# Two graph-attention and expert layers on one core: the first layer's row terms sent through DRAM, and two of four norms taken from accumulator sums and squares on ScalarE

## The chip, the cores and the metric

The kernel runs on one core of one Trainium2 chip, as one launch. The metric is the device time of that launch in microseconds (us). The kernel before took 1596.94 us (the median of three runs, 1593.39 to 1600.9). One further execution was taken with the hardware profiler; every line number, duration and wait below comes from it.

Five engines are named as in the profile: PE (TensorE, with its weight load PEld), DVE (VectorE), ACT (ScalarE), POOL (GpSimd) and SP (SyncE, which here only issues transfers). Each executes its own instructions in the order in which they were recorded.

## What is computed

x holds 64 batches of 256 rows with 256 features, float32. The adjacency (256 x 256) is the same for all batches. Two layers follow each other; cut to what matters:

```python
# layer 0: attention of 4 heads (64 wide), then a linear map
h = layernorm(x);  q = (h @ W).reshape(B, N, 4, 64)
e = leaky(e_src[:, :, None, :] + e_dst[:, None, :, :], 0.2)   # e_src, e_dst = q @ a
attn = softmax(where(adj > 0, e, -9e15), axis=2)
x = x + elu(einsum('bijh,bjhd->bihd', attn, q))
x = x + layernorm(x) @ weight.T + bias
# layer 1: attention of 1 head, then a mixture of 8 experts, 2 per row
x = x + relu(softmax(mask(leaky(...))) @ (layernorm(x) @ W))
t = layernorm(x);  top-2 experts of t @ router_w.T
x = t + sum over the two of weight * (gelu(t @ w1 + b1) @ w2 + b2)
```

The softmax weights need no exponential of a 256 x 256 matrix: exp(leaky(s + d)) is a maximum of two products, so each entry of the weights is max(row term, column term) times the mask, and the denominator comes from a column of ones-like terms in the product with q. The row terms of a head are 256 numbers that every partition needs: one number for each row i, the same on all 128 partitions (which carry j). How these numbers get to all partitions is the first thing changed here. The mean and the variance of the four layernorms of a batch are the second.

## The kernel before

**Work of a batch.** `batch_layers` (line 509) is a Python generator: it records the instructions of one batch in some twenty pieces, and between two pieces it yields a rank. A loop at the end of the file (line 1112 on) goes through steps. In every step it takes each active generator once, in the order of the ranks that they yielded, and lets it record its next piece; a negative rank means a further piece in the same step. Three steps (`TICKS = 3`) are one period, and a new batch begins in each period, so in a steady state one period holds one complete batch's work, made up of pieces of some seven batches. The recorded order is the order on every engine; nothing reorders it later. Engines wait for each other only by semaphores.

**Order of a batch's pieces (before):** blocks of x turned on DVE (L116); norm of x (L374, L375, finished on POOL by L382 and L383); projection on PE (L405) and exponentials on ACT (L413); `scaled` on DVE (L421) in the same step; in the next two steps `scores` for heads 0, 1 and heads 2, 3; then `attended` on PE (L496); the head products divided (on ACT, L534, for batches under `EARLY = 16`, else on DVE, L539); the ELU: `e` on ACT (L545), x1 on DVE (L548, L549); x1b (L552: POOL for the early batches, else DVE); norm of x1, transposed on PE (L389) and copied by ACT (L395); the linear map on PE (L560) and x2 on DVE (L566); norm of x2; transposed, copied, projected for layer 1 (L440), ACT exponentials (L447, L448, L453); scores of layer 1 (L459, L464), attention (L496), `rel` on ACT (L582); x2 += rel on DVE (L586); its norm; normalised rows on ACT (L603, L608), stored by SP (L619), transposed, router logits on PE (L633). A batch's routing and its experts follow in other generators: rows are scattered to DRAM by POOL (L933), read back in pairs of 128 rows by SP (L767, L793), turned (L116 sT), multiplied (L825), passed through gelu on ACT (L831), multiplied again (L840), biased on DVE (L850), weighted on ACT (L818) and added to the output by POOL (L861). Three batches at the end take a dense way.

**Row terms before.** `scores` (line 469) lets PE transpose a column of q that is broadcast along the free axis, once for each head and half (L475, eight 128 x 128 transposes for a batch, in two groups of four). The result lies in a PSUM bank `pd` on all partitions. DVE then forms the weights `z` of a head and a half from `pd`, a column of q and the mask (L482, eight instructions of 128 x 256 for a batch).

**Norms before.** `norm_stats` (line 360) issues two BATCH_NORM_STATS2 (L374) and two BATCH_NORM_AGGREGATE (L375) on DVE for each of the four norms of a batch. Two norms that fall into one step share one pair of POOL instructions, which add EPS and raise to the power -1/2 (`finish_norms`, L382 and L383).

**Transfers.** In the steady state all are issued by SP and POOL; ACT issues six at the start and none after. Every transfer takes one of eight completion semaphores in turn, and waits for the transfer that had it before.

Of the kernel before, what the change touches and what calls it, by code (L numbers as in the profile page):

```python
# [9 lines left out]
F32 = mybir.dt.float32  # L10
# [5 lines left out]
P = 128  # L16
# [11 lines left out]
def kernel(  # L28
# [83 lines left out]
    S = 32  # L112

# [270 lines left out]

    def transposed(src, pool=work, tag="xT", bufs=4, blocks=False):
        pt = bank("pt", [KT, N])
        for t in range(NT):
            for k in range(KT):
                nc.tensor.transpose(  # L389
                    pt[:, k, t * P : (t + 1) * P],  # L390
                    by_block(src[:, t, :])[:, k] if blocks else src[:, t, k * P : (k + 1) * P],
                    ident,
                )
        dst = pool.tile([P, KT, N], F32, tag=tag, name="xT", bufs=bufs)
        nc.scalar.copy(dst, pt)  # L395
        return dst
# [59 lines left out]
    def scores1(ex, me):  # L456
        pd = bank("pd", [N])
        for t in range(NT):
            nc.tensor.transpose(  # L459
                pd[:, t * P : (t + 1) * P], ex[:, t, 1:2].to_broadcast([P, P]), ident  # L460
            )
        z = work.tile([P, NT, N], F32, tag="z", name="z", bufs=6)
        for j in range(NT):
            nc.vector.scalar_tensor_tensor(  # L464
                z[:, j, :], pd, ex[:, j, 2:3], me[:, j, :], op0=ALU.max, op1=ALU.mult
            )
        return z

    def scores(q, heads, hs, mask, probs):

        d = D // heads
        pd = bank("pd", [len(hs), N])
        for i, h in enumerate(hs):
            for t in range(NT):
                nc.tensor.transpose(  # L475
                    pd[:, i, t * P : (t + 1) * P],
                    q[:, t, h, d + 1 : d + 2].to_broadcast([P, P]), ident,
                )
        for i, h in enumerate(hs):
            z = work.tile([P, NT, N], F32, tag="z", name="z", bufs=6)  # L480
            for j in range(NT):
                nc.vector.scalar_tensor_tensor(  # L482
                    z[:, j, :], pd[:, i, :], q[:, j, h, d + 2 : d + 3], mask[:, j, :],
                    op0=ALU.max, op1=ALU.mult,
                )
            probs.append(z)

    def attended(q, heads, probs):
# [3 lines left out]
        for t in range(NT):  # L492
            pv = bank("pv", [heads, d + 1])
            for h, z in enumerate(probs):
                for j in range(NT):
                    nc.tensor.matmul(  # L496
                        pv[:, h, :], z[:, j, t * P : (t + 1) * P], q[:, j, h, : d + 1],
                        start=(j == 0), stop=(j == NT - 1),
                    )
# [6 lines left out]
    def batch_layers(b, c0, xng, lg):  # L506
# [13 lines left out]
        scaled(q, pqs, H, rstd)  # L520
        yield 10
        probs = []
        scores(q, H, range(0, 2), masks[0], probs)
        yield 10
        scores(q, H, range(2, 4), masks[0], probs)
        yield 50
        pvs, rinv = attended(q, H, probs)
# [36 lines left out]
        x2 = work.tile([P, NT, D], F32, tag="x2", name="x2", bufs=4)  # L564
        for t in range(NT):
            nc.vector.scalar_tensor_tensor(  # L566
                x2[:, t, :], pf[:, t, :], rstd[:, t : t + 1], x1b[:, t, :],
                op0=ALU.mult, op1=ALU.add,
            )
        _, rstd = norm_stats(x2)  # L570
# [7 lines left out]
        pvs, rinv = attended(q[:, :, None, :], 1, [z])  # L578
        yield 5
        rel = work.tile([P, NT, D], F32, tag="rel", name="rel", bufs=1)  # L580
        for t, pv in enumerate(pvs):
# [4 lines left out]
        nc.vector.tensor_add(x2, x2, rel)  # L586
        mv, rstd = norm_stats(x2)
        yield 15
# [3 lines left out]
            by[:, 0], mv[:, :, 0], -1.0, rstd, op0=ALU.mult, op1=ALU.mult  # L592
# [512 lines left out]
    with tc.manual_schedule():  # L1105
        while more or active or waiting or dense_jobs or scatters:
# [35 lines left out]
            if half_done:  # L1142
                finish_norms(NT)
            active[:] = [a for a in active if a[0] is not None]
# [36 lines left out]
```

## Time and profile before

| | |
|---|---|
| median of three runs | 1596.94 us (1593.39 to 1600.9) |
| the profiled execution: its time, its span | 1597.13 us, 1595.3 us |
| mean granted PE clock | 0.977 |
| transfers | 207.58 MB, 361512 packets |
| L475 transposes of q, PE | 512, busy 77.5 us |
| L482 z, DVE | 512, 473 ns each |
| L374, L375 of all four norms, DVE | 512 each, busy 156.2 + 50.5 and 93.1 us |
| L545 e, ACT | 64, 642 ns each |
| ACT table loads of 1283 ns | 66 + 49 + 6 + 4 + 3 + 3 + 1 |

Busy time counts the time in which an engine executes; register, semaphore and transfer-issuing instructions are not in it. Instructions that overlap on one engine are counted once within a group, and groups of one engine can overlap each other, so the groups' busy times add up to more than the engine's. In the timeline a row gives the start, the length, engine, line, operation, the tile written and read, the count of merged instructions, and in brackets the engine's idle time ahead of it and what ended it. "SPq" and "ACTq" rows are the issuing of transfers on these engines' queues.

### The profile page before, as it was taken

Reading aid. Unit: us, or ns where it says so; the run is one execution under the profiler, and the core shown is the slowest. Engines: PE = TensorE matmul, PEld = TensorE weight load, DVE = VectorE, ACT = ScalarE, POOL = GpSimd, SP = SyncE. Lnnn points to the kernel's source line nnn. Section 1 sums busy time; section 2 is a strip of 40 time slices with the busy share of each in tenths; the row PEclk is TensorE's granted clock in tenths of the full one; section 3 lists DMA queues with packets and bytes.
Section 4 is the critical chain, followed back from the end, with each engine's and each line's share of the span. In section 5 each row is a group of like instructions: output and inputs, shape, how many; then the busy total and the mean of one; then the engine's idle time right before and its main releaser. Section 6 shows DMA issues by size and latency. Waiting matters only on the chain. (4 is left out here: it accounts for less than half of the span.)

```text
span 1595.3 us, 30506 instructions
## 1 busy us (share of the span) xinstructions
PE 1493.9 (94%) x8570; PEld 1317.6 (83%) x8570; DVE 1325.8 (83%) x4473; ACT 902.8 (57%) x2003; POOL 903.3 (57%) x867
## 2 busy tenths in 40 slices
PE   6998888999999999999999999999898997769998
PEld 5887777888888888888888888888787886658886
DVE  6898988989898989898998989899898889655553
ACT  2455455466666656666665666666466776544332
POOL 2332636265757666666757575756755575654443
PEclk9999998999999999999999999999999999889999
DMA  5712223456666667565666666666576665678863
GB/s 160 207 50 55 85 73 90 116 134 140 133 140 144 132 149 147 121 148 131 153 130 154 132 131 138 144 140 139 124 160 128 124 143 105 134 187 164 155 120 47
DMA packets 361512, 207.58 MB, mean 130 GB/s; under 512 B 261497, under 2 KB 331649, under 8 KB 361345
## 3 DMA queue, kind: packets, MB, share of 16 engines
q1 hardware_dynamic: 311488, 138.31, 35.6%
q0 software_dynamic: 48864, 66.33, 22.8%
q8 instruction: 71, 1.16, 0.3%
q10 hardware_dynamic: 992, 0.99, 0.2%
q14 instruction: 97, 0.79, 0.2%
HBM read 117.43 MB, written 88.09 MB: 129 GB/s over the span
## 5 line engine op out<-in xcount | busy, mean ns | idle before, releaser
L861 POOL DMA_INDIRECT out_dram<-y,xt x258 | 411.8, 1596 | 182.1 <-ACT hT L831 50.5
L496 PE MATMUL pv<-q,z 128*128 128x65 f32 (+1 forms) x2560 | 372.8, 301 | 5.7 <-issue 4.4
L496 PEld LDWEIGHTS pv<-q,z 128*128 128x128 f32 x2560 | 333.9, 194 | 19.1 <-issue 4.6
L840 PE MATMUL py<-w2s,hT 128*128 (+1 forms) x1224 | 283.5, 383 | 7.8 <-ACT hT L831 6.5
L382 POOL TENSOR_SCALAR rstd<-mv 128x4 f32<-128x4 f32 (+1 forms) x132 | 57.0, 432 | 411.0 <-DVE mv L375 365.0
L933 POOL DMA_INDIRECT xs<-xng,pos x244 | 247.7, 1015 | 65.4 <-issue 63.1
L840 PEld LDWEIGHTS py<-w2s,hT 128*128 128x128 f32 x1224 | 229.6, 192 | 40.4 <-ACT hT L831 9.3
L395 ACT COPY xT<-pt 128x512 f32<-128x512 f32 x192 | 113.4, 591 | 253.9 <-PE pt L389 189.6
L825 PE MATMUL ph<-sT,we 128*128 128x256 f32 x1032 | 241.1, 384 | 10.9 <-DVE sT L116 10.0
L825 PEld LDWEIGHTS ph<-sT,we 128*128 128x128 f32 x1032 | 193.5, 193 | 36.9 <-DVE sT L116 10.8
L482 DVE SCALAR_TENSOR_TENSOR z<-pd,q,mask 128x256 f32<-128x256 f32 x512 | 210.9, 473 | 0.0
L831 ACT ACTIVATE hT<-ph,we 128x256 f32<-128x256 f32 x306 | 127.7, 470 | 143.0 <-PE ph L825 120.0
L818 ACT ACTIVATE y<-y,w 128x256 f32<-128x256 f32 x258 | 112.5, 500 | 135.8 <-DVE y L850 115.2
L383 POOL TENSOR_TENSOR rstd<-rstd,mhalf 128x4 f32<-128x4 f32 (+1 forms) x132 | 161.2, 1221 | 11.0
L374 DVE BATCH_NORM_STATS2 stats<-x 128x6 f32<-128x256 f32 x384 | 156.2, 407 | 2.2
L440 PE MATMUL pq<-wx,xT 128*128 128x259 f32 x512 | 129.5, 394 | 24.3 <-ACT xT L395 13.0
L405 PE MATMUL pq<-wx,xT 128*128 128x268 f32 x512 | 132.8, 404 | 5.7 <-DVE xT L116 3.8
L850 DVE TENSOR_TENSOR y<-py,b2s 128x512 f32<-128x512 f32 x129 | 85.9, 686 | 60.6 <-PE py L840 44.9
L440 PEld LDWEIGHTS pq<-wx,xT 128*128 128x128 f32 x512 | 91.7, 189 | 51.6 <-ACT xT L395 22.7
L560 PE MATMUL pf<-wfT,xT 128*128 128x256 f32 x512 | 123.3, 384 | 0.1
L405 PEld LDWEIGHTS pq<-wx,xT 128*128 128x128 f32 x512 | 98.3, 196 | 24.8 <-issue 3.2
L375 DVE BATCH_NORM_AGGREGATE mv<-stats 128x2 f32<-128x6 f32 x512 | 93.1, 182 | 17.5
(159 smaller groups left out, 2339.7 us busy)
## 6 DMA issues: line engine op xcount, KB each, us to landing
we<-wpack SPq DMA_DIRECT2D x145, 288.0 KB
xr<-xs SPq DMA_DIRECT2D x516, 64.0 KB
xblk<-in_x_dram SPq DMA_DIRECT2D x256, 64.0 KB
xin<-in_x_dram SPq DMA_DIRECT2D x64, 256.0 KB
out_dram<-base SPq DMA_DIRECT2D x61, 256.0 KB
out_dram<-y,xt POOLq DMA_INDIRECT x258
xs<-xng,pos POOLq DMA_INDIRECT x244
xs<-fill SPq DMA_DIRECT2D x9, 260.0 KB
```

The lines of the kernel that those rows point to most:

```text
L374: nc.vector.bn_stats(stats[:, t, :], src[:, t, :])
L383: nc.gpsimd.tensor_tensor(rstd[:, :n], rstd[:, :n], mhalf[:, :n], ALU.pow)
L405: nc.tensor.matmul(pq.rearrange("p h c -> p (h c)"), xT[:, k, t * P : (t + 1) * P], wx[:, k, :], start=(k == 0), stop=(k == KT - 1),)
L440: nc.tensor.matmul(pq, xT[:, k, t * P : (t + 1) * P], wx1[:, k, :], start=(k == 0), stop=(k == KT - 1),)
L482: nc.vector.scalar_tensor_tensor(z[:, j, :], pd[:, i, :], q[:, j, h, d + 2 : d + 3], mask[:, j, :], op0=ALU.max, op1=ALU.mult,)
L496: nc.tensor.matmul(pv[:, h, :], z[:, j, t * P : (t + 1) * P], q[:, j, h, : d + 1], start=(j == 0), stop=(j == NT - 1),)
L560: nc.tensor.matmul(pf[:, t, :], xT[:, k, t * P : (t + 1) * P], wfT[:, k, :], start=(k == 0), stop=(k == KT - 1),)
L825: nc.tensor.matmul(ph[:, f, :], we[:, k * D + f * P : k * D + (f + 1) * P], xT[:, k, :], start=(k == 0), stop=(k == KT - 1),)
L831: nc.scalar.activation(hT[:, f, :], ph[:, f, :], AF.Gelu, bias=we[:, C_B1 + f : C_B1 + f + 1])
L840: nc.tensor.matmul(py[:, t, :], hT[:, f, t * P : (t + 1) * P], w2s[:, e, f * D : (f + 1) * D].rearrange("p e c -> p (e c)"), start=(f == 0 ...
L861: d = nc.gpsimd.indirect_dma_start(out=out_rows, out_offset=bass.IndirectOffsetOnAxis(ap=xt[:, t, 0:1].bitcast(I32), axis=0), in_=y[:, t, ...
L933: d = nc.gpsimd.indirect_dma_start(out=xs_d[: E * CAP * PAIR, :], out_offset=bass.IndirectOffsetOnAxis(ap=at, axis=0), in_=xe, in_offset=None,
```

## The change

In layer 0 the row terms no longer pass through PE. `send_terms`: DVE transposes the 32 columns that hold them (4 for each of 8 head-halves) in blocks of 32 x 32 into `ut`; ACT issues a transfer of the 32 rows that matter, 128 bytes each, to a small DRAM tile, 4 KB for a batch. Two steps later `spread_terms`: ACT issues one transfer that reads these 4 KB for each of the 128 partitions, 512 KB in SBUF, into the second half of a new tile `z4` (two buffers). Two steps after that `scores` runs, now with both large operands in SBUF: it multiplies in place, the last half over the row terms themselves. Between `scaled` and `scores` there are four steps in place of one, so all later pieces of a batch are recorded one period later relative to its projection; the program has three steps more.

The norm of x2 and that after x2 += rel no longer use BATCH_NORM_STATS2. The DVE instructions that produce x2 now also give the sum of each row (`accum_out`), the addition of `rel` is split into two halves for it, and ACT computes Square(sum - 256 x) with an accumulator for each half: four activations of 128 x 256 for a batch, which write their elements into one scratch tile `off` with one buffer. POOL turns the accumulators into 1/sqrt as before, with its own pairing. `by` is formed from the sums, and is recorded at rank 80 instead of 15. The other two norms (of x and of x1) stay as they were.

On ACT the four squares come, in the recorded order, after the copy of the transposed normalised rows (L395, xT<-pt) and ahead of `e` (L545); the transfer of the terms is issued right behind the squares. The spreading transfer is issued behind the copy of the transposed x1. On PE the two groups L475 vanish and nothing else moves within a period.

```diff
+    G = P // S
+    def norm_squares(src, sums):
+        ...
+        for t in range(NT):
+            off = work.tile([P, D], F32, tag="off", name="off", bufs=1)
+            nc.scalar.activation(
+                off, src[:, t, :], AF.Square, bias=sums[:, t : t + 1], scale=-float(D),
+                accum_out=sq[:, at + t : at + t + 1],
+            )
+        if at:
+            finish_squares(2 * NT)
+        return rstd[:, at : at + NT]
+
+    def finish_squares(n):
+        sq, rstd = half_squared.pop()
+        nc.gpsimd.tensor_scalar(
+            rstd[:, :n], sq[:, :n], 1.0 / D**3, EPS, op0=ALU.mult, op1=ALU.add
+        )
+        nc.gpsimd.tensor_tensor(rstd[:, :n], rstd[:, :n], mhalf[:, :n], ALU.pow)
...
+    def send_terms(q, b):
+        ut = small.tile([P, S], F32, tag="ut", name="ut", bufs=1)
+        nc.vector.transpose(
+            ut.rearrange("p (t h w) -> p t h w", t=NT, h=H), q[:, :, :, HD - 1 : HD + 3]
+        )
+        ud = tc.dram_tile([S, S], F32, name=f"terms_{b}")
+        ud = ud.rearrange("c r -> (c r)").rearrange("(c p) -> c p", p=P)
+        return ut, ud
+
+    def spread_terms(ud):
+        z = work.tile([P, NT, NT, H, P], F32, tag="z4", name="z4", bufs=2)
+        nc.scalar.dma_start(
+            out=z[:, NT - 1].rearrange("p t h i -> p (t h i)"),
+            in_=rows_to_all(ud, S * S),
+        )
         return z
 
-    def scores(q, heads, hs, mask, probs):
-        pd = bank("pd", [len(hs), N])
-        for i, h in enumerate(hs):
-            for t in range(NT):
-                nc.tensor.transpose(
-                    pd[:, i, t * P : (t + 1) * P],
-                    q[:, t, h, d + 1 : d + 2].to_broadcast([P, P]), ident,
-                )
-        for i, h in enumerate(hs):
-            z = work.tile([P, NT, N], F32, tag="z", name="z", bufs=6)
+    def scores(q, z, hs):
+        for h in hs:
             for j in range(NT):
                 nc.vector.scalar_tensor_tensor(
-                    z[:, j, :], pd[:, i, :], q[:, j, h, d + 2 : d + 3], mask[:, j, :],
+                    z[:, j, :, h, :], z[:, NT - 1, :, h, :], q[:, j, h, HD + 2 : HD + 3],
+                    masks[0][:, j, :].rearrange("p (t i) -> p t i", t=NT),
                     op0=ALU.max, op1=ALU.mult,
                 )
...
         scaled(q, pqs, H, rstd)
+        ut, ud = send_terms(q, b)
+        yield -75
+        nc.scalar.dma_start(
+            out=ud.rearrange("c (g r) -> g c r", g=G),
+            in_=ut[2 : P : S // (NT * H), :],
+        )
+        yield 99
+        yield 30
+        z = spread_terms(ud)
+        yield 99
         yield 10
-        probs = []
-        scores(q, H, range(0, 2), masks[0], probs)
+        scores(q, z, range(0, 2))
         yield 10
-        scores(q, H, range(2, 4), masks[0], probs)
+        scores(q, z, range(2, 4))
         yield 50
...
         x2 = work.tile([P, NT, D], F32, tag="x2", name="x2", bufs=4)
+        sums = row_sums()
         for t in range(NT):
             nc.vector.scalar_tensor_tensor(
                 x2[:, t, :], pf[:, t, :], rstd[:, t : t + 1], x1b[:, t, :],
-                op0=ALU.mult, op1=ALU.add,
-            )
-        _, rstd = norm_stats(x2)
+                op0=ALU.mult, op1=ALU.add, accum_out=sums[:, t : t + 1],
+            )
+        rstd = norm_squares(x2, sums)
...
-        nc.vector.tensor_add(x2, x2, rel)
-        mv, rstd = norm_stats(x2)
-        yield 15
+        sums = row_sums()
+        for t in range(NT):
+            nc.vector.scalar_tensor_tensor(
+                x2[:, t, :], x2[:, t, :], 1.0, rel[:, t, :],
+                op0=ALU.mult, op1=ALU.add, accum_out=sums[:, t : t + 1],
+            )
+        rstd = norm_squares(x2, sums)
+        yield 80
...
-            by[:, 0], mv[:, :, 0], -1.0, rstd, op0=ALU.mult, op1=ALU.mult
+            by[:, 0], sums, -1.0 / D, rstd, op0=ALU.mult, op1=ALU.mult
```

More of the change, by code (lines that the diff above doesn't have):

```diff
@@ L383, in finish_norms, with row_sums @@
         nc.gpsimd.tensor_tensor(rstd[:, :n], rstd[:, :n], mhalf[:, :n], ALU.pow)
+    half_squared = []
+    def row_sums():
+        return small.tile([P, NT], F32, tag="sums", name="sums", bufs=8)
+    def norm_squares(src, sums):
+        if half_squared:
+            sq, rstd = half_squared[0]
+            at = NT
+        else:
+            sq = small.tile([P, 2 * NT], F32, tag="sq", name="sq", bufs=4)
+            rstd = small.tile([P, 2 * NT], F32, tag="rstd", name="rstd", bufs=5)
+            half_squared.append((sq, rstd))
+            at = 0
+        for t in range(NT):
[13 more added lines that the diff above has]
+        nc.gpsimd.tensor_tensor(rstd[:, :n], rstd[:, :n], mhalf[:, :n], ALU.pow)
     def transposed(src, pool=work, tag="xT", bufs=4, blocks=False):
@@ L461, in scores1 @@
             )
-        z = work.tile([P, NT, N], F32, tag="z", name="z", bufs=6)
+        z = work.tile([P, NT, N], F32, tag="z1", name="z1", bufs=1)
         for j in range(NT):
@@ L466, in scores1, with attended @@
             )
-        return z
-    def scores(q, heads, hs, mask, probs):
-        d = D // heads
-        pd = bank("pd", [len(hs), N])
-        for i, h in enumerate(hs):
-            for t in range(NT):
-                nc.tensor.transpose(
-                    pd[:, i, t * P : (t + 1) * P],
-                    q[:, t, h, d + 1 : d + 2].to_broadcast([P, P]), ident,
-                )
-        for i, h in enumerate(hs):
-            z = work.tile([P, NT, N], F32, tag="z", name="z", bufs=6)
+        return [z[:, j, :] for j in range(NT)]
+    def send_terms(q, b):
[12 more added lines that the diff above has]
+        )
+        return z
+    def scores(q, z, hs):
+        for h in hs:
             for j in range(NT):
                 nc.vector.scalar_tensor_tensor(
-                    z[:, j, :], pd[:, i, :], q[:, j, h, d + 2 : d + 3], mask[:, j, :],
+                    z[:, j, :, h, :], z[:, NT - 1, :, h, :], q[:, j, h, HD + 2 : HD + 3],
+                    masks[0][:, j, :].rearrange("p (t i) -> p t i", t=NT),
                     op0=ALU.max, op1=ALU.mult,
                 )
-            probs.append(z)
-    def attended(q, heads, probs):
+    def attended(q, heads, z):
         d = D // heads
@@ L493, in attended @@
             pv = bank("pv", [heads, d + 1])
-            for h, z in enumerate(probs):
+            for h in range(heads):
                 for j in range(NT):
                     nc.tensor.matmul(
-                        pv[:, h, :], z[:, j, t * P : (t + 1) * P], q[:, j, h, : d + 1],
+                        pv[:, h, :], z(j, h, t), q[:, j, h, : d + 1],
                         start=(j == 0), stop=(j == NT - 1),
@@ L520, in batch_layers @@
         scaled(q, pqs, H, rstd)
+        ut, ud = send_terms(q, b)
[8 more added lines that the diff above has]
+        yield 99
         yield 10
-        probs = []
-        scores(q, H, range(0, 2), masks[0], probs)
+        scores(q, z, range(0, 2))
         yield 10
-        scores(q, H, range(2, 4), masks[0], probs)
+        scores(q, z, range(2, 4))
         yield 50
-        pvs, rinv = attended(q, H, probs)
+        pvs, rinv = attended(q, H, lambda j, h, t: z[:, j, t, h, :])
         hp = work.tile([P, NT, D], F32, tag="hp", name="hp", bufs=1)
@@ L577, in batch_layers @@
         yield 40
-        pvs, rinv = attended(q[:, :, None, :], 1, [z])
+        pvs, rinv = attended(
+            q[:, :, None, :], 1, lambda j, h, t: z[j][:, t * P : (t + 1) * P]
+        )
         yield 5
@@ L1143 @@
                 finish_norms(NT)
+            if half_squared:
+                finish_squares(NT)
             active[:] = [a for a in active if a[0] is not None]
```

## The prediction

> **What bounds the kernel now.** I first read the shares and slices of the page.
>
> ```profile
> PE 1493.9 (94%) x8570; PEld 1317.6 (83%) x8570; DVE 1325.8 (83%) x4473; ACT 902.8 (57%) x2003; POOL 903.3 (57%) x867
> PE   6998888999999999999999999999898997769998
> ```
>
> PE fills most slices, but not slices 3 to 6 (120 to 280 us) and not the end. So I took the windows by stage (PE, PEld, DVE, ACT, POOL busy, clock):
>
> ```profile
> 87.00:101.00 14.00, 13.76 (x91) 12.25 (x90) 12.37 (x40) 8.10 (x25) 4.64 (x6) 1.00 0.21 58
> 160.00:200.00 40.00, 36.29 (x218) 31.57 (x219) 36.31 (x119) 18.91 (x55) 25.10 (x28) 0.96 0.26 81
> 600.00:800.00 200.00, 197.85 (x1198) 177.43 (x1197) 179.46 (x592) 123.18 (x266) 131.45 (x123) 1.00 0.64 140
> 1213.80:1240.90 27.10, 24.76 (x144) 21.86 (x143) 23.08 (x78) 20.44 (x38) 15.75 (x15) 1.00 0.53 112
> ```
>
> There are three stages. From 320 to 1114 us lie 37 periods (starts of the L405 group on PE) of 21.3 to 21.7 us with 0.24 us of PE idle each: PE sets them. The 16 early batches (to about 290 us) take 13.3 to 21.8 us each, with DVE as busy as PE. The eight last periods (24 to 30 us) have both waiting on each other. Which wait ends last is then read from the timeline of one period of each stage. Steady, PE and ACT:
>
> ```profile
> 799.81 0.60 PE L475 MATMUL pd<-ident,q 128*128 128x128 f32 x4
> 800.25 3.62 PE L825 MATMUL ph<-sT,we 128*128 128x256 f32 x16
> 806.34 0.60 PE L389 MATMUL pt<-ident,x 128*128 128x128 f32 x4
> 806.77 0.60 PE L475 MATMUL pd<-ident,q 128*128 128x128 f32 x4
> 807.61 2.02 PE L440 MATMUL pq<-wx,xT 128*128 128x259 f32 x8 [0.24 <-issue]
> 806.97 0.58 ACT L395 COPY xT<-pt 128x512 f32<-128x512 f32 x1 [2.23 <-PE pt L389]
> ```
>
> One L475 group is followed at once by other work, 0.44 us later. The other stands where PE must wait anyway: L440 needs the copy xT, which ACT can begin only when pt is done (806.94). Early, ACT, DVE and POOL:
>
> ```profile
> 92.79 1.74 ACT L534 ACTIVATE hp<-pv,rinv 128x64 f32<-128x64 f32 x8 [0.87 <-DVE rinv L503]
> 94.37 0.64 ACT L395 COPY xT<-pt 128x512 f32<-128x512 f32 x1
> 94.83 0.70 ACT L545 ACTIVATE e<-hp 128x512 f32<-128x512 f32 x1
> 97.39 0.69 DVE L549 SCALAR_TENSOR_TENSOR x<-e,x 128x512 f32<-128x512 f32 x1
> 98.95 1.27 POOL L552 TENSOR_TENSOR x1b<-x,bias_f 128x512 f32<-128x512 f32 x1
> 99.57 0.67 DVE L591 SCALAR_TENSOR_TENSOR by<-mv,rstd 128x2 f32<-128x2 f32 x1
> ```
>
> `e` ends at 95.53; L549 reads it 1.86 us later, because DVE is still at the norms. That 1.86 us is all the slack that ACT has there.
>
> **The sum** is made against the profiled execution, 1597.1 us (span 1595.3 and 1.8 around it), 0.2 us above the median of the runs.
>
> **Removed from PE: 512 transposes.** Their busy time is 77.5 us, but what returns is less. Steady: the first group gives 0.44 us. The second gives nothing: pt, copy, L440 stay one chain, and L475's place becomes idle. 37 x 0.44 = **-16**. Early: PE is not what will set the period (below), so 0.
>
> **The four squares of a batch, S.** No row shows Square with an accumulator. Nearest rows on 128 x 256: two `rel` in 0.84 us (0.42 each) below; `xng` 0.61 plus a separate small instruction for the accumulator, `warm` 0.20, above. So S is 1.7 to 3.25 us. They share one scratch tile and wait for each other, so I take the `me` row, 0.52, and 0.13 for wait and accumulator: **S = 2.6**. Square needs no table of its own: the built program has 134 loads where 132 were.
>
> **Early batches.** Behind the squares on ACT stands `e`, and for `e` waits L549 on DVE, behind which stands everything DVE does: scores, turning x, norms, then the q and rinv that the next hp needs. This is a closed chain through DVE and ACT. Now hp to L549 takes 4.60 us, set by DVE. After: the copy ends at 95.01, squares from 94.9 to 97.5, `e` to 98.2, L549 at 98.3: +0.9. The turning of ut, ahead of rinv on DVE, adds 0.15 (DVE's small rows are 0.13 to 0.2). DVE's saving of the norms, between rinv and L549, falls into the wait. 16 x 1.05 = **+17**. With S = 1.7, +0.15 each (+2); with 3.25, +1.7 (+27).
>
> **z from SBUF.** L482 with PSUM input advances 0.41 each (four in 1.65); SBUF-only instructions of 512 elements advance 0.61 to 0.73 (L549, L552 back to back), so half that, 0.31 to 0.47. I take no change; ends -0.8 and +0.5 us per batch. But L591 above, two columns wide, took 0.67 where its like take 0.15: it has two SBUF tensors, and ended (100.24) with POOL's L552 (100.22). L482 beside it, with PSUM, was not held. After the change the first scores stand beside L552 in early batches and would be held for its 1.27 us instead of 0.5. Half of the early batches already lose as much to small routing instructions there, so 8 x 0.75 = **+6** (0 to +16).
>
> A Trainium skill rule speaks against these instructions. The "Vector Engine (DVE) Microarchitecture Reference", section "Points that are easy to get wrong", says that this instruction kind with two non-bf16 SBUF sources runs at half throughput, no port being left for the accumulator. L548 (two float32 SBUF sources, no accumulator) takes 659 ns for 512 elements against 676 for the plain addition L586, so the row shows no halving. As an estimate from that page's rule, eight scores would cost about 2 us more a batch, some +30 us over the early batches. I go by the row.
>
> **Norms on DVE.** Gone: four L374 and four L375, 4 x (0.41 + 0.18) = 2.4 us of a batch. L586 becomes two halves, +0.15 to +0.5; accumulators 0 to 0.16 each on four instructions. DVE saves some 1.3 to 2 us a batch. Steady: DVE already waits for PE there (5.3 us over four periods, rinv and y), so nothing comes back. Could ACT be late? pf ends at 799.97, x2's halves and squares end by 802.2 to 802.9, `e` 802.9 to 803.5 (L549 now: 803.49, so DVE loses nothing), table load and four hT (2 x 0.84) 805.9 to 806.6; the copy is wanted at 806.5. It just fits; beyond S = 3.2, every 0.1 us costs 3.7 us of the run.
>
> **Last eight periods.** PE waits 1.4 to 2.9 us each, in 1213 to 1241 us 2.18 us for ACT's copy. ACT there waits 3.72 us for y on DVE, which stands behind both norms. The squares fit into that wait, and y comes 2 us sooner. I take 0.75 us each, **-6** (-12 to +3).
>
> **One period more.** The last batch is followed by as many steps as now (29), so the cost lies at the fill, where a first period is worth 6.0 us (11.94 to 17.97) to 11.1 (to 29.08). With ACT's transfers queued beside the weight packing I take **+8** (+3 to +14).
>
> **Hidden.** ACT issues two transfers a batch, 0.33 to 0.54 us each; at 1.85 us in the trace such an issue runs inside ACT's table load, so I take 0 (0.9 us of ACT uncovered). 512 KB per batch take 2.5 us at the best slice (207 GB/s) and 4 us at the mean (130); the scores come two steps, some 14 us, later. Behind a late transfer all of DVE would stand. SP's transfers now take turns with ACT's on the completion semaphores, so one SP load a period waits for a spread to land: issued behind ACT's third copy (811.94), landed by 814.5 to 817, the load behind it by 818 to 821 (2.5 to 4 us for each, as above), and L825 wants it at 821.2 or, for the second pair, 823: 0 to 5 us to spare. POOL: 133 pairs instead of 132.
>
> Sum: -16 +17 +6 -6 +8 = +9, hence **1606 us**, slightly slower.
>
> **Rivals.**
>
> Faster: S is near 1.7 and `e` still meets DVE in time. Then early +2, lock +2, steady -16, last -8, fill +5: 1582. For it: the 1.86 us of slack and 0.42 rows; against: the shared scratch tile, which forbids overlap. It decides below S = 2.0. Chance 0.2.
>
> ACT becomes the bound: S of 3.6 (and issue not hidden). Early 16 x 2.05 + 6 = 39, steady 0, last -2, fill 8: 1642. For: accumulator reads as separate instructions; against: ACT is now 57% busy. Chance 0.15.
>
> PE gains nothing: the freed 0.44 us becomes one more wait. Early +23, steady 0, last -3, fill 8: 1625. Chance 0.15.
>
> Spread or SP's load late by 1 us a steady period: 1606 + 37 = 1643. Against: DMA is 64% busy, with 14 us of lead. Chance 0.08.
>
> **Numbers.** Forecast 0.42 (1598 to 1616). Within 0.5%, about what a measurement can tell from no change, means 1589 to 1605: about 0.2, nearly all of it from the forecast's lower half. Faster by more, 0.2 (the first rival); slower by more, 0.6 (the forecast's upper half and the other three). Leaving out the worst of both sides, the range is 1576 to 1645.
>
> **What will show it.** Early: L549's successor waits for ACT `e`, and its distance from hp is 5.5 us or more. Steady: period 20.9 us with PE idle of some 0.8 between pt and L440. Squares: S read directly. Scores in early batches with one long row beside POOL's L552. It would be wrong if an accumulator costs a second instruction of 0.3 us, or if the early chain is broken by an order on DVE that I misread.

## The result and the profile after

The changed kernel takes 1604.62 us, the median of 5 runs (1603.38 to 1605.76), beside 1597.08 us for the kernel before (the median of 5 runs): a ratio of 1.0047, with a 95% interval of 1.0028 to 1.0065. The profiled execution took 1603.38 us with a span of 1601.6 us. The forecast was 1606 us, so the total came out as predicted; the parts did not all. The difference of 0.47% is about the size that a measurement of this kernel can tell from none; the interval says that it is there.

First the page of the changed kernel: the shares and PE's and ScalarE's slices.

```profile
PE 1447.8 (90%) x8058; PEld 1269.7 (79%) x8058; DVE 1241.7 (78%) x4345; ACT 1054.3 (66%) x2517; POOL 873.6 (55%) x869
PE   4888888799999999999999999999899998869996
ACT  1466657567777777777777777777568888654331
```

512 PE instructions and 46.1 us of its busy time are gone, DVE has 84.1 us less and ACT 151.5 us more. Yet PE's slices 1 to 3 and 8 are lower than before (4, 8, 8 and 7 against 6, 9, 9 and 9): in the early stage it now has more holes, not fewer. The windows by stage (PE, PEld, DVE, ACT, POOL busy, clock, DMA share, GB/s), one early period first, then as before:

```profile
97.20:113.90 16.70, 13.89 (x89) 12.00 (x88) 12.31 (x40) 11.31 (x35) 4.10 (x7) 1.00 0.26 79
160.00:200.00 40.00, 33.73 (x207) 29.34 (x206) 31.17 (x114) 24.63 (x78) 14.24 (x18) 0.96 0.26 84
600.00:800.00 200.00, 193.92 (x1141) 173.28 (x1140) 169.24 (x582) 146.99 (x346) 131.13 (x127) 1.00 0.74 171
1218.30:1244.30 26.00, 25.67 (x146) 22.62 (x145) 21.18 (x79) 22.28 (x44) 12.40 (x12) 1.00 0.64 135
```

In 160 to 200 us both PE (36.3 to 33.7) and DVE (36.3 to 31.2) lost busy time, while ACT gained (18.9 to 24.6): the rows below show that DVE now waits for ACT. From 600 to 800 us PE has a little idle time, though the periods are shorter.

To see in which stage the time went, I mark four points on DVE: the first x1 (the last addition of `e`, L549 before and L601 after), the x1 of batch 17, that of batch 53, and the span's end. Every kernel of this study is cut at the same four places (us):

| kernel | first x1 | early (batch 0 to 17) | steady (17 to 53) | 53 to end | profiled span |
|---|---|---|---|---|---|
| before | 26.2 | 285.1 | 770.4 | 513.7 | 1595.3 |
| after | 34.2 | 304.5 | 756.7 | 506.2 | 1601.6 |
| difference | +8.0 | +19.4 | -13.6 | -7.5 | +6.3 |

The early stage, in rows of the changed kernel's timeline (DVE, POOL, ACT; in brackets the idle time ahead and what ended it):

```profile
97.86 2.81 DVE L525 SCALAR_TENSOR_TENSOR z<-z,q,mask 128x256 f32<-128x256 f32 x4
98.03 1.44 POOL L604 TENSOR_TENSOR x1b<-x,bias_f 128x512 f32<-128x512 f32 x1
101.41 0.13 DVE L651 SCALAR_TENSOR_TENSOR by<-sums,rstd 128x2 f32<-128x2 f32 x1
101.53 1.92 DVE L525 SCALAR_TENSOR_TENSOR z<-z,q,mask 128x256 f32<-128x256 f32 x4
108.59 1.75 ACT L586 ACTIVATE hp<-pv,rinv 128x64 f32<-128x64 f32 x8 [1.09 <-DVE rinv L546]
110.66 0.58 ACT L402 ACTIVATE off<-x,sums 128x256 f32<-128x256 f32 x1
113.05 0.19 ACT L402 ACTIVATION_READ_ACCUMULATOR off<-x,sums 128x1 f32 x1
113.21 0.63 ACT L597 ACTIVATE e<-hp 128x512 f32<-128x512 f32 x1
113.88 0.69 DVE L601 SCALAR_TENSOR_TENSOR x<-e,x 128x512 f32<-128x512 f32 x1 [2.80 <-ACT e L597]
```

Three things are to be seen. The four squares run from 110.66 to 113.2 (2.55 us, each followed by a separate read of its accumulator), and `e` stands behind them, so DVE waits 2.80 us. The four scores beside POOL's x1b take 2.81 us, and the four without it 1.92; before, 1.65 and 1.63. And `by`, 0.67 us before, is 0.13 now, since it runs only after x1b has ended (99.47). That holds for the first of these batches; in four later ones, with routing work on POOL ahead of x1b, `by` still meets it and takes 1.4 to 1.55 us.

The steady stage, PE and ACT:

```profile
824.03 1.98 PE L539 MATMUL pv<-q,z 128*128 128x257 f32 x8
825.85 0.60 PE L421 MATMUL pt<-ident,x 128*128 128x128 f32 x4
826.49 0.59 ACT L427 COPY xT<-pt 128x512 f32<-128x512 f32 x1 [0.99 <-PE pt L421]
827.13 2.02 PE L472 MATMUL pq<-wx,xT 128*128 128x259 f32 x8 [0.68 <-ACT xT L427]
```

PE waits 0.68 us between pt and L472, where the second group of transposes used to lie, and ACT, with the squares done, still waits 0.99 us for pt.

### The profile page after: what moved, and what is told of

It reads as the page before. It is cut to its first block, busy times and chain, and to the rows that moved or that the text cites. A ratio compares the mean times of both kernels' runs of the same rounds, so it can differ in the third digit from the quotient of the medians.

```text
span 1601.6 us, 30115 instructions
## 1 busy us (share of the span) xinstructions
PE 1447.8 (90%) x8058; PEld 1269.7 (79%) x8058; DVE 1241.7 (78%) x4345; ACT 1054.3 (66%) x2517; POOL 873.6 (55%) x869
## 5 line engine op out<-in xcount | busy, mean ns | idle before, releaser
L539 PEld LDWEIGHTS pv<-q,z 128*128 128x128 f32 x2560 | 335.2, 195 | 20.7 <-issue 4.5
L993 POOL DMA_INDIRECT xs<-xng,pos x244 | 258.6, 1060 | 65.4 <-issue 59.6
L525 DVE SCALAR_TENSOR_TENSOR z<-z,q,mask 128x256 f32<-128x256 f32 x512 | 244.7, 499 | 9.2
L472 PE MATMUL pq<-wx,xT 128*128 128x259 f32 x512 | 136.5, 411 | 59.0 <-ACT xT L427 38.1
L878 ACT ACTIVATE y<-y,w 128x256 f32<-128x256 f32 x258 | 113.2, 503 | 110.0 <-DVE y L910 97.1
L891 ACT ACTIVATE hT<-ph,we 128x256 f32<-128x256 f32 x306 | 124.0, 474 | 63.9 <-PE ph L885 47.9
L472 PEld LDWEIGHTS pq<-wx,xT 128*128 128x128 f32 x512 | 96.2, 198 | 87.7 <-ACT xT L427 46.7
L402 ACT ACTIVATE off<-x,sums 128x256 f32<-128x256 f32 x256 | 132.0, 516 | 48.7 <-DVE x L643 21.4
L437 PE MATMUL pq<-wx,xT 128*128 128x268 f32 x512 | 135.3, 410 | 13.6 <-DVE rinv L546 5.6
L910 DVE TENSOR_TENSOR y<-py,b2s 128x512 f32<-128x512 f32 x129 | 85.7, 687 | 59.5 <-PE py L900 37.3
L412 POOL TENSOR_SCALAR rstd<-sq 128x4 f32<-128x4 f32 (+1 forms) x66 | 13.2, 201 | 214.4 <-ACT off L402 214.0
L383 POOL TENSOR_SCALAR rstd<-mv 128x4 f32<-128x4 f32 (+1 forms) x67 | 15.7, 234 | 208.4 <-DVE mv L376 165.3
L437 PEld LDWEIGHTS pq<-wx,xT 128*128 128x128 f32 x512 | 99.5, 199 | 34.0 <-issue 10.6
L601 DVE SCALAR_TENSOR_TENSOR x<-e,x 128x512 f32<-128x512 f32 x64 | 44.3, 693 | 86.0 <-ACT e L597 83.9
```

The source lines that it names most:

```text
L402: nc.scalar.activation(off, src[:, t, :], AF.Square, bias=sums[:, t : t + 1], scale=-float(D), accum_out=sq[:, at + t : at + t + 1],)
L437: nc.tensor.matmul(pq.rearrange("p h c -> p (h c)"), xT[:, k, t * P : (t + 1) * P], wx[:, k, :], start=(k == 0), stop=(k == KT - 1),)
L472: nc.tensor.matmul(pq, xT[:, k, t * P : (t + 1) * P], wx1[:, k, :], start=(k == 0), stop=(k == KT - 1),)
L525: nc.vector.scalar_tensor_tensor(z[:, j, :, h, :], z[:, NT - 1, :, h, :], q[:, j, h, HD + 2 : HD + 3], masks[0][:, j, :].rearrange("p (t i ...
L539: nc.tensor.matmul(pv[:, h, :], z(j, h, t), q[:, j, h, : d + 1], start=(j == 0), stop=(j == NT - 1),)
L891: nc.scalar.activation(hT[:, f, :], ph[:, f, :], AF.Gelu, bias=we[:, C_B1 + f : C_B1 + f + 1])
```

## The experiments

Theory at the start: the loss of the early batches (+19.4) comes from the squares ahead of `e`, as the prediction had it. Rival: it comes from the row terms, whose scores are read from SBUF. The first four kernels were to tell these apart. Each kernel below has one profile, so its times by stage are one execution's; medians and ratios are of all its runs.

**The row terms alone.** The changed kernel with every norm by statistics:

```diff
-                op0=ALU.mult, op1=ALU.add, accum_out=sums[:, t : t + 1],
-            )
-        rstd = norm_squares(x2, sums)
+                op0=ALU.mult, op1=ALU.add,
+            )
+        _, rstd = norm_stats(x2)
...
+        nc.vector.tensor_add(x2, x2, rel)
+        mv, rstd = norm_stats(x2)
+        yield 15
...
```

> The row terms over DRAM of the changed kernel, with every norm taken by VectorE's statistics as before. In the changed kernel the early batches cost 19.4 us more than before (first x1 to the x1 of batch 17). Theory 1, the squares ahead of e cause it: without them VectorE no longer waits 2.8 us for e, and only the dearer scores and the transpose of the terms stay, about +0.2 us a batch: fill +8, early +3, steady part -12, last part -1, so -2 against before: 1595 us. Rival, the row terms cause it (scores read from SBUF, held by GpSimd's bias addition, four in 2.8 us against 1.65): early +17, so +12 against before: 1609 us. Both at once in equal parts would give about 1602.

Measured: 1616.25 us (its runs lie between 1609.92 and 1626.62), 1.0142 times before (1.0109 to 1.0174); early 301.8 us, steady 759.2. That is slower than the rival asked for, and the theory's 1595 us is refuted. In its timeline (DVE) nothing waits for `e`; the scores are the long rows:

```profile
98.99 0.69 DVE L601 SCALAR_TENSOR_TENSOR x<-e,x 128x512 f32<-128x512 f32 x1
99.60 2.81 DVE L525 SCALAR_TENSOR_TENSOR z<-z,q,mask 128x256 f32<-128x256 f32 x4
103.30 1.89 DVE L525 SCALAR_TENSOR_TENSOR z<-z,q,mask 128x256 f32<-128x256 f32 x4
110.07 0.21 DVE L505 STREAM_TRANSPOSE ut<-q 128x32 f32<-128x32 f32 x1
```

Against the 1.65 and 1.63 us of before, that is 1.16 + 0.26 us for the scores and 0.14 to 0.21 for turning ut, in an engine that is busy for 89.3 of 100 us from 100 to 200 us (89.9 before), more than PE with 85.4.

**The norms alone.** The kernel before with the sums and squares:

```diff
+                op0=ALU.mult, op1=ALU.add, accum_out=sums[:, t : t + 1],
+            )
+        rstd = norm_squares(x2, sums)
-        _, rstd = norm_stats(x2)
...
```

> The norms by accumulator sums and squares of the changed kernel, with the row terms transposed on TensorE as before. Theory 1, the squares ahead of e cause the loss of the early batches: no fill, early +13 (the addition that waits for e starts some 0.8 us later in each of 16 batches), steady part 0 (VectorE's saving lies in its wait for TensorE), last part -6: +7 against before, 1604 us. Rival, the row terms cause the loss: early +2, so -4 against before: 1593 us. If VectorE's time sets the steady part after all, it is lower by 1.3 us in each of 37 periods: under 1560 us.

Measured: 1581.46 us, 0.9923 (0.9903 to 0.9943): faster than before, and faster than either theory said. Early 283.6 us (-1.5), steady 770.0 (-0.3), 53 to end 497.0 (-16.7). DVE does wait for `e`, and it costs nothing (ACT and DVE):

```profile
108.20 1.75 ACT L565 ACTIVATE hp<-pv,rinv 128x64 f32<-128x64 f32 x8 [0.87 <-DVE rinv L534]
113.38 0.69 DVE L580 SCALAR_TENSOR_TENSOR x<-e,x 128x512 f32<-128x512 f32 x1 [1.96 <-ACT e L576]
101.52 0.13 DVE L628 SCALAR_TENSOR_TENSOR by<-sums,rstd 128x2 f32<-128x2 f32 x1
```

From hp to this addition it is 5.18 us, 0.58 more than the 4.60 before; but `by`, which the change also moves behind the turning of x, is 0.54 us shorter because POOL's x1b is over by then. The two cancel in the batches without routing work: a period is 14.77 to 14.86 us there, and 14.52 to 14.87 before. In the mean of 15 early batches hp to the addition is 4.98 us against 4.64, and from the addition to the next hp 10.74 against 11.07; in five of the later batches `by` meets x1b and takes 1.7 to 1.9 us, so what shortens the second stretch there is not `by` and was not taken apart. The rest of DVE's saving (busy 89.9 of 100 us from 100 to 200 us before, 76.3 here) is spent waiting.

**`e` first.** The changed kernel with the squares one step later, right behind `e`:

```diff
-        rstd = norm_squares(x2, sums)
-        yield 60
+        yield 6
+        rstd = norm_squares(x2, sums)
+        yield -60
...
-        rstd = norm_squares(x2, sums)
-        yield 80
+        yield 6
+        rstd = norm_squares(x2, sums)
+        yield -80
+        if half_squared:
+            finish_squares(NT)
```

> The changed kernel with the four squares behind e on ScalarE instead of ahead of it, everything else in its order. Theory 1, the place of the squares causes the loss of the early batches: VectorE's 2.8 us wait for e falls to some 0.4 us, the squares then delay the copy of the transposed x1 by about 0.5 us, so an early period (16.6 us after the change) loses some 2 us: 16 times is -32, and the loss of 19.4 bounds the part that is the squares' own: between 1573 and 1586 us. Rival, the row terms cause the loss: the wait moves to the scores behind it, less than 5 us in all: 1600 us or more.

Measured: 1582.03 us, 0.9916 (0.9897 to 0.9935); early 277.1 us, 27.4 less than with the squares first and 24.7 less than with the row terms alone; steady 756.7 as before. This is inside the theory's range. In one early period (DVE) the wait for `e` is 0.24 us, against 2.80 before this edit, and the long scores are still there:

```profile
108.22 0.69 DVE L601 SCALAR_TENSOR_TENSOR x<-e,x 128x512 f32<-128x512 f32 x1 [0.24 <-ACT e L597]
108.83 2.82 DVE L525 SCALAR_TENSOR_TENSOR z<-z,q,mask 128x256 f32<-128x256 f32 x4
```

So both theories hold for a part: the row terms cost, and the squares ahead of `e` swallow a relief of DVE that would have paid for it.

**x1b on VectorE**, so that GpSimd does not work beside the scores:

```diff
-        eng = nc.gpsimd if early else nc.vector
+        eng = nc.vector
```

> The changed kernel with the bias addition x1b of the early batches on VectorE too, so that GpSimd never works beside the first scores. Theory 1 (the squares ahead of e are the main loss): four scores go from 2.81 to 1.91 us, and VectorE does one addition of 0.6 us itself: -0.3 us in each of 16 batches, -5: 1600 us. Rival, GpSimd's hold on the scores is the main loss of the early batches: -15 or more, 1590 us. If the early period is bounded elsewhere: no change, 1605 us.

Measured: 1596.76 us, 1.0010 (0.9993 to 1.0027); early 298.9 us, -5.6 against the changed kernel. As theory 1 said: GpSimd's hold costs, but taking it away for 0.69 us of DVE returns little.

**The norms with `e` first, terms turned on TensorE** (both edits above on the kernel before):

> The terms transposed on TensorE as before the change, the norms by sums and squares, and the squares behind e. Theory: the relief of VectorE by the sums is eaten in the early batches by its wait for e (with the norms alone the early part took 283.6 us against 285.1 before, although VectorE had 2.1 us less to do in each batch). With e first, VectorE's 15.0 us of work and some 0.6 us of other waits bound an early period of 17.2 us: -1.3 each, some -20: 1561 us. Rival, TensorE bounds the early batches as soon as VectorE is relieved (it is busy 91 of 100 us there): not more than -5, 1576 to 1584 us.

Measured: 1563.28 us, 0.9804 (0.9777 to 0.9832); early 261.3 us, -22.3 against the norms alone. The theory's 1561 us was right to 2 us. DVE's waits in one early period are now these:

```profile
93.12 0.48 DVE L598 SCALAR_TENSOR_TENSOR x<-pf,rstd,x1b 128x256 f32<-128x256 f32 x1 [1.39 <-PE pf L591]
94.74 0.69 DVE L580 SCALAR_TENSOR_TENSOR x<-e,x 128x512 f32<-128x512 f32 x1
95.34 1.65 DVE L513 SCALAR_TENSOR_TENSOR z<-pd,q,mask 128x256 f32<-128x256 f32 x4
```

It waits 1.39 us for PE's pf, no longer for `e`. With 93.2 of 100 us busy from 100 to 200 us, TensorE is the likely next bound of this stage; no run tests that. A second run of the same kernel, beside the last experiment below, gave the same:

> A second run of the kernel with the terms transposed on TensorE, the norms by sums and squares and e first, beside the kernel with the row terms in the middle alone, to compare the two directly: 1561 to 1566 us as before, and its part behind batch 53 within 3 us of 495.7 us if one profile is enough to tell that part; a spread of 8 us or more would leave the difference of the last part open.

Measured: 1563.44 us, 0.9789 (0.9773 to 0.9804); early 261.6, steady 770.4, 53 to end 499.6 against 502.2. (The expectations count the last part to the last row of PE, DVE, ACT or POOL, my table to the span's end, some 6.5 us later.) So these two profiles agree to 3 us in the last part. Others do not: the four kernels, above and below, that have `e` first and the row terms in all batches from 16 on record the same instructions there, and their last parts are 506.1, 509.8, 512.9 and 513.3 us, their steady ones 753.7 to 760.8. So two profiles alone do not show a difference of less than some 7 us in these parts.

**By stage.** The first 16 batches turned on TensorE, later ones over DRAM, `e` first:

```diff
+        if b < EARLY:
+            yield 10
+            z = work.tile([P, NT, NT, H, P], F32, tag="z4", name="z4", bufs=2)
+            scores_turned(q, z, range(0, 2))
+            yield 10
+            scores_turned(q, z, range(2, 4))
+        else:
+            ut, ud = send_terms(q, b)
...
```

> Batches 0 to 15 with the terms transposed on TensorE into PSUM, as before the change; later batches with the terms over DRAM; norms by sums and squares with the squares behind e. Theory, the losses of the row terms (fill, dearer early scores) and their gain (steady part) are separable by batch: fill and early part as in the kernel with the norms and e first, steady part -12 against that kernel, and 0 to 8 us for the one period in which batch 16 comes later: some 1545 to 1560 us, and 5 to 14 us under that kernel. Rival, the extra period costs as much at batch 16 as at the fill and the late order undoes the rest: no better than that kernel.

Measured: 1572.93 us, 0.9842 (0.9813 to 0.9872): the rival. Up to batch 15 its periods are those of the kernel before it, and its steady part is 16.7 us shorter; but the two periods in which batch 16 comes later take 27.40 and 25.09 us instead of 19.71 and 15.93. The inserted period costs 16.8 us here, twice the fill, of which some 4 us seem to come back later (the steady part of the next kernel, with the same code there, is 757.8 us against 753.7). And the last part is 10.6 us longer. (The runs of this kernel lie between 1563.88 and 1574.1 us, and its interval overlaps that of the norms with `e` first, 0.9777 to 0.9832: it is no better, and that it is worse is not sure.)

**The delay without the row terms.** As by stage, but the early batches also wait a period, so that nothing is inserted at batch 16:

```diff
         if b < EARLY:
+            yield 99
+            yield 30
+            yield 99
             yield 10
```

> As the kernel by stage (batches 0 to 15 transposed on TensorE into PSUM, later ones over DRAM, squares behind e), but the early batches take their scores a period later too, so that no period is inserted at batch 16. Theory 1, the early loss of the row terms is the price of the scores read from SBUF beside GpSimd's addition and of turning the terms, and a period of delay costs its fill alone: fill +7.5 against the kernel with the norms and e first, early part as there (261 us), nothing lost at batch 16, steady part -14, last part 0 to +8: 1557 to 1565 us. Rival, the later order itself makes the early batches dearer: early part 275 us or more, 1570 us or above.

Measured: 1566.86 us, 0.9798 (0.9778 to 0.9818); first x1 at 34.4 us (+6.8), early 260.0, steady 757.8, 53 to end 513.3. Theory 1 holds for the early part: a period's delay costs its fill, and what the row terms cost there is theirs: the scores from SBUF, the turning and what these trigger. The undisturbed early period is 14.42 us with the delay as without it. The last kernel below has the same code there, and its early part is 267.9 us; so a cost of the delay of up to 7 us in the first period and in those with routing work is not excluded. The scores here read PSUM and write the same tile `z4` as those over DRAM, and neither the tile nor GpSimd's addition beside them makes them longer (DVE, POOL):

```profile
103.30 1.66 DVE L542 SCALAR_TENSOR_TENSOR z<-pd,q,mask 128x256 f32<-128x256 f32 x4
103.47 1.28 POOL L632 TENSOR_TENSOR x1b<-x,bias_f 128x512 f32<-128x512 f32 x1 [6.56 <-DVE x L629]
```

So the place of the row terms makes the scores dearer, not the layout of what they write. In all the delayed, split kernel is no faster than the one without row terms over DRAM (0.9804). The time lies 2 us above the range, by the last part.

**`e` first and x1b on VectorE together:**

> The changed kernel with e ahead of the squares and x1b of the early batches on VectorE, so that GpSimd never works beside the first scores. Theory 1, VectorE's own time bounds the early batches once e is first: four scores beside x1b go from 2.80 to 1.92 us, the addition itself takes VectorE 0.69, so -0.2 in each of 16 batches: -3, 1579 us. Rival 1, GpSimd's hold reaches further than the scores: -10 or more, 1572 us or less. Rival 2, something else bounds them: within 2 us of 1582.

Measured: 1577.40 us, 0.9864 (0.9844 to 0.9883). The time fits theory 1; the early part of its profile, 277.1 us, is that of `e` first, which speaks for rival 2. The profiled execution is the slowest of the four (1582.21 us), so this stays open.

**Two more squares**, in batches 24 to 55 of the changed kernel:

```diff
+        if 24 <= b < 56:
+            more_sq = small.tile([P, 2 * NT], F32, tag="more_sq", name="more_sq", bufs=1)
+            for t in range(NT):
+                off = work.tile([P, D], F32, tag="off", name="off", bufs=1)
+                nc.scalar.activation(
+                    off, x2[:, t, :], AF.Square, bias=sums[:, t : t + 1], scale=-float(D),
+                    accum_out=more_sq[:, t : t + 1],
+                )
```

> The changed kernel with two more squares with accumulators of x2 on ScalarE in batches 24 to 55, whose results nothing reads; it adds work and leaves none out. Measured, two cost 1.27 us of ScalarE. Theory, ScalarE has 0.99 us to spare in a steady period (its wait for pt ahead of the third copy): 0.28 us in each of 32 periods come on top, +9: 1614 us. Rival 1, ScalarE has more to spare, since other waits give way: no change, 1605 us. Rival 2, ScalarE has nothing to spare and its work stands in the path: 32 times 1.27 us, +40: 1645 us.

Measured: 1618.98 us, 1.0155 (1.0120 to 1.0189): 14.4 over the changed kernel by the medians, 17 by the ratios to the kernel before; steady +16.9. Nearest the theory of +9, but the mean hides a pattern. The periods come in fours: before the edit 20.7, 21.3, 20.5 and 21.5 us, with it 20.8, 21.3, 20.8 and 22.8. Three of four take 1.27 us of ACT nearly whole into slack; the fourth, where DVE's x is late, has almost none. ACT and PE in that one:

```profile
828.33 0.51 ACT L402 ACTIVATE off<-x,sums 128x256 f32<-128x256 f32 x1 [1.93 <-DVE x L651]
834.02 1.57 ACT L899 ACTIVATE hT<-ph,we 128x256 f32<-128x256 f32 x4
835.46 0.60 ACT L427 COPY xT<-pt 128x512 f32<-128x512 f32 x1
836.12 2.02 PE L472 MATMUL pq<-wx,xT 128*128 128x259 f32 x8 [2.09 <-ACT xT L427]
```

The third copy follows hT at once, without the wait for pt that it has in the changed kernel, and PE waits 2.09 us instead of 0.68.

**No period for the transfers.** The spread right behind the write, the scores one step later:

```diff
-        yield 99
-        yield 30
         z = spread_terms(ud)
-        yield 99
         yield 10
```

> The changed kernel with the spreading read issued right behind the write of the terms, and the scores one step later as before the change, not a period later. Theory, the period hides the transfers: ScalarE then waits for the terms to land ahead of e, and VectorE for the spread ahead of the scores, 2 to 4 us in each of 64 periods less the fill's 8: +100 or more, over 1700 us. Rival, the transfers are hidden without the period (0.99 us to spare on ScalarE, VectorE 85% busy): the 8 us of the fill come back, 1597 us.

Measured: 1825.32 us, 1.1450 (1.1410 to 1.1490). The cover is worth 220 us: DVE's scores (a group of all 64 batches) and ACT in the period at 700 us show where it was,

```profile
L525 DVE SCALAR_TENSOR_TENSOR z<-z,q,mask 128x256 f32<-128x256 f32 x512 | 237.5, 485 | 156.1 <-DMA z<-terms 146.9
717.81 0.32 ACTq L515 DMA_DIRECT2D z<-terms  x1
718.18 0.63 ACT L594 ACTIVATE e<-hp 128x512 f32<-128x512 f32 x1 [3.04 <-DMA xr<-xs]
```

2.3 us a batch before the scores. In the period at 700 us ACT stands 3.04 us ahead of `e`; the profile names a load of SP for this wait, but the spread's issue, which needs the terms in DRAM, stands ahead of `e` and goes out as the wait ends. Over the run 74.0 us of ACT's idle time ahead of `e`, in 43 periods, are put down to the terms. The granted clock fell too, from 0.972 over the changed kernel's span to 0.920, and how much of the 220 us that makes was not separated. In the changed kernel the scores' idle time is 9.2 us over the whole run.

**The row terms in the middle alone**, batches 16 to 52; all batches a period later, `e` first:

```diff
-        if b < EARLY:
+        if b < EARLY or b >= 53:
```

> All batches take their scores a period later; only batches 16 to 52 have their terms over DRAM, the first 16 and the last 11 are transposed on TensorE into PSUM; squares behind e. In four kernels with the row terms and the new norms the part behind batch 53 took 8 to 11 us more than in the kernels with the new norms alone (for example 506.7 against 495.7 us). Theory 1, that is again the price of the scores read from SBUF, where VectorE and TensorE wait for each other: the last part falls to some 496 us, the time to 1557 us. Rival, it comes from the later order or from the write of the terms by other means: the last part stays at 503 to 507 us, the time at 1564 to 1570 us.

Measured: 1558.36 us, 0.9744 (0.9723 to 0.9765), beside 0.9789 (0.9773 to 0.9804) for the norms with `e` first run side by side with it. The two intervals do not touch. The last part is 496.0 us, where theory 1 put it, against 506.1 to 513.3 in the four kernels with the row terms in it and `e` first. It is the fastest of the study, 2.6% under the kernel before. (Its early part, 267.9 us, is longer than the 260.0 us of the same code above, in the first period and in three with routing work; the steady one is 756.7.) PE shows what became of its saving there. In the ten periods behind batch 53 it has some 80 instructions less with the row terms, but it waits for 17.8 to 22.4 us (six profiles with the new norms), against 9.0 to 12.5 us in the four without row terms there, most of it ahead of layer 1's projection, for the copy xT by ACT. And its granted clock is lower in these periods, 0.94 to 0.97 against 0.99, while its busy time is about the same (232 to 240 us against 236 to 241). How much is the waits' and how much the clock's was not separated.

## Why the prediction was right, and where it was not

The early stage in all its versions, as first x1 to the x1 of batch 17 (us):

| | statistics on DVE | squares ahead of `e` | `e` first |
|---|---|---|---|
| terms turned on TensorE | 285.1 | 283.6 | 261.3 |
| terms over DRAM | 301.8 | 304.5 | 277.1 |

Down a column are the row terms: +16.7, +20.9, +15.8. From the first to the last column is the relief by the sums: -23.8 and -24.7. From the last to the middle one is the place of the squares: +22.3 and +27.4. The loss of 19.4 is 16.7 - 24.7 + 27.4, or, added in the other order, -1.5 + 20.9. The early parts of the same code repeat to 0.5 us in two pairs of profiles and differ by 8 us in a third, so every one of these differences stands clear of that but the -1.5. The ratios of whole runs agree: the row terms cost 1.0142 against 1, 1.0047 against 0.9923 and 0.9916 against 0.9804, some 18 to 23 us each time.

- **PE's transposes (-16).** Right. An undisturbed period goes from 21.33 to 20.89 us and from 21.78 to 21.34 (both kernels with `e` first): 0.44, and the second group of four became the idle time before L472. Over 36 periods 13.6 us came back in the changed kernel, of 15.8 if every one gave it. The rival in which PE gains nothing is out.
- **S (2.6 us).** Right, 2.55 in early batches: 516 ns each and 192 ns for a separate accumulator read, 0.63 to 0.64 us from one to the next. The accumulator does cost a second instruction, but of 0.19 us, not of the 0.3 us that would have been a sign against the forecast. The faster rival, with S near 1.7, is out; so is the slower one with 3.6.
- **Early batches, `e` behind the squares (+17).** This is the step that failed, in its attribution. The wait is there, but smaller: 5.29 us from hp to the addition, short of the "5.5 us or more" that was asked for, so 0.7 us in place of 0.9. And the same norms, in the batches without routing work, also took 0.54 us from `by`, which I had seen held by POOL's x1b and did not count as removed. The norms alone therefore cost nothing in this stage (-1.5, against a forecast of 16 x 0.9 = 14). And "DVE's saving of the norms falls into the wait" is true only of this order: with `e` first the saving is worth some 24 us. I priced the wait and not what stood behind it.
- **Scores from SBUF ("no change") and held by POOL (+6, 0 to +16).** Mis-sized: the row terms alone cost 16.7 us here, against the 6 of this term and the 16 x 0.15 = 2.4 for ut in the term above. The hold is as described (2.81 us for four). But the unheld four also rose, from 1.63 to 1.92 us, +0.26 to +0.29 for four, and so about the upper bound of +0.5 for the eight of a batch, not the zero that I took. Together with ut it is 1.6 us in a period without routing, and 16.7 us are 1.04 us in the mean of 16. With `e` first it lies where the scores stand: from the addition to the next hp 11.81 us in the mean of 15 batches, against 10.71 with the terms turned on TensorE, while hp to the addition stays (3.56 and 3.66). The rule of the Trainium skill's page "Vector Engine (DVE) Microarchitecture Reference" (section "Points that are easy to get wrong") stays unconfirmed: the scores with both sources in SBUF take 0.48 us from one to the next against 0.39 with one in PSUM, not twice as much, and x2's halves with two SBUF sources and an accumulator take 417 ns for 256 elements, against 676 ns for the plain addition of 512 before.
- The two errors cancel: +17 and +6 were forecast, and +19.4 was measured, of which the row terms alone are nearly the whole. That the total came within 2 us of 1606 us is, in this stage, luck.
- **Norms off DVE, ACT just fits.** Right in the steady part: the norms alone change it by 0.3 us. The threshold of S = 3.2 and 3.7 us of the run for each 0.1 beyond is somewhat too steep: an S of 3.82 us would cost 20 us over 32 periods by it and cost 14 to 17, about 0.5 in the mean of one, most of it in the one period of four that has no slack.
- **Last periods (-6).** The size came out (-7.5), but is about as large as the spread of this part between profiles, and it hid two terms: the norms give -16.7 alone, and the row terms take back 2 to 9 us (513.7 to 515.7; 497.0 to 506.2). With `e` first the last part is 499.6 and 502.2 us without the row terms, 496.0 in the last kernel, and 506.1 to 513.3 with them: some 10 us. The forecast had no cost of theirs in this stage, though DVE and PE wait for each other there. PE's added waits stand ahead of layer 1's projection, at a lower granted clock (above); which instruction of the row terms makes the copy late was not isolated. (Not all of these periods take 24 to 30 us, as I read: one of PE's is 21.8.)
- **One period at the fill (+8).** Right: +8.0 between the two profiles. Over all profiles the first x1 is at 26.0 to 28.3 us without the delay and at 34.2 to 37.3 with it (37.0 in the kernel without a period for the transfers). That a delay costs little but the fill is shown by the late turned batches (early 260.0 against 261.3, though 267.9 in the second profile of that code).
- **Hidden transfers (0).** Right: 9.2 us of idle time before all scores. Late transfers showed only with the period gone, and then cost 220 us.

## What to carry to other kernels

When an engine is relieved, ask what the work does on the engine that takes it: here the squares stood ahead of the one instruction that the relieved engine waits for, and a move of one step was worth 22 and 27 us of the early stage. A change of two parts should be priced in a table of both, stage by stage; a total near zero may be a gain and a loss that a different order keeps apart. And an edit that pays in the stage that TensorE bounds can cost in those where VectorE is as busy: here, of the splits that were run, the row terms paid best in batches 16 to 52 alone.

## What the hardware showed that I had not expected

- A ScalarE square with a sum is two instructions, 516 and 192 ns; on VectorE the accumulator's read is 84 ns and costs 0.04 us from one instruction to the next (x2's two halves start 0.41 us apart in the changed kernel, 0.37 us before, without accumulators).
- A score of 128x256 elements takes 0.39 us from one to the next with its first operand in PSUM and 0.48 with it in SBUF, where GpSimd's addition is not beside it. Beside that addition of two SBUF tensors four of them take 2.81 instead of 1.92 us with the operand in SBUF, and 1.65 us as ever with it in PSUM.
- An issue of a DMA by ScalarE (0.53 us at 821.40) lies inside a square (821.39 to 821.90) and costs little, though not the nothing that was assumed: from the start of this last square to `e` it is 0.58 us, and 0.51 us in the kernel with the norms alone, which has no issue there.
- The granted clock differs between stages and kernels: in the first 40 us it was 0.96 before, with TensorE 27.2 us busy, and 0.91 in the changed kernel with 19.7; from 600 to 800 us it was 1.00 in both, but 0.91 in the kernel without a period for the transfers, whose TensorE was busy for 176.8 of these 200 us against 193.9. It does not follow the busy time alone: 0.84 in the first 40 us with x1b on VectorE and TensorE 22.9 us busy, more than the 19.7 above.
